# A transformer block with a selective scan: one of two convolved chunks goes from VectorE to TensorE, and steps of the hand-written schedule are placed elsewhere

## Chip, cores and metric

The kernel runs on one core of a Trainium2 chip. The metric is the device time of one execution in microseconds. TensorE, VectorE, ScalarE, GpSimd and SyncE are called PE, DVE, ACT, POOL and SP, as in the profile; PEld is PE's loading of weights. The five engines each work through a queue of their own, in order, and wait for each other by semaphores.

## What is computed

Four sequences of 256 tokens with 512 features go through two layers. The first layer (latent attention beside a gated feed-forward) is untouched by the change. The second layer adds a selective state-space block and a mixture of low-rank experts to its input:

```python
proj = hidden_states @ in_proj_w                 # 512 -> 2 x 1024
x, z = jnp.split(proj, 2, axis=-1)               # both then [batch, 1024, 256]
xp = jnp.pad(x, ((0, 0), (0, 0), (K - 1, 0)))    # K = 4
xc = conv_b[None, :, None]
for k in range(K):
    xc = xc + conv_w[None, :, k:k+1] * xp[:, :, k:k+Lq]
xc = silu(xc)
ssm_p = einsum('bdl,ed->ble', xc, x_proj_w)      # -> dt_r (32), B (16), C (16), each normalised
dt = softplus(einsum('blr,dr->bdl', dt_r, dt_proj_w) + dt_bias)
# scan over time: h = exp(dt * A) * h + dt * B * x ;  y = sum_n h * C
y = (ys + D_param * xc) * silu(z)
out = einsum('bdl,hd->blh', y, out_proj_w)
```

The experts' part is a dense product of the same normalised input, a router (softmax over 8 experts, the two best kept) and rank-16 products weighted by it. The part in question is the convolution: four taps along time, with one weight per channel and tap.

## The kernel before

The first layer fills the first 40% of the time and is bound by PE. Its last products run into the beginning of the scan.

**Tiling of the second layer.** The 1024 channels are eight chunks `c` of 128 partitions; two chunks form a pair `p`. The 16 states of a chunk are taken in four groups, so a chunk has four *steps* and a sequence `PER` = 32. Step `u` of 128 belongs to sequence `u // 32`; `u % 32` is called its place below.

**One step.** ACT forms the decays of step `u + 2` (`decays`, four instructions on L930, into one of three buffers); DVE multiplies the B rows with dt·x (`scan_in`, bx on L936) and scans (`scan`, h on L951); POOL multiplies h with the C rows (hc on L955, in the same function); PE sums the states of step `u - 1` into `ysum` (`states_sum`, L967, with the D part on L965 first in each chunk). Two steps after a chunk's last step DVE closes it (`close_chunk`, L971): `ysum` times the SiLU of z, written over the chunk's `xc`. There are two buffers of h, three of hc, one `ysum`.

**Side work.** While sequence `b` is scanned, the next one, `nxt`, is prepared. Small functions do this, each put to a place by hand: `put(b, place, function, ...)` lists it ahead of the place's scan, `put_late` behind it. Within an engine the order of these lists is the order of the queue. They are: `norm_*` (layer norm), `px_mm` (product with the x half of `in_proj_w`, L737), `conv_in` and `conv_taps` (the convolution of a pair), `conv_silu` (SiLU over all eight chunks, and of a z gate), `pp_mm`, `pp_square`, `pp_norm` (the projection to dt, B and C and its norm), `step_in`, `step_exp`, `step_out` (softplus of dt), `step_x` (dt times x), `spread` (dt and dt·x out to DRAM and back in another layout), `c_rows` and `b_rows`. For sequence `b` itself there are `pz_mm` (z product, L898) with `gate_silu`, and every second sequence `router`, `route_exp`, `route`. For the block's output there are `dense`, `expert_out`, `expert_turn`, `out_mm` (one chunk of `out_proj`, L1059) and `out_x`, which copies the result on ACT and has SP store it; the second half of a sequence's rows is finished early in the next sequence, the first half through the next sequence's places 4 to 15.

**The convolution of a pair.** `conv_in` works on ACT: it copies the product `px` into a padded buffer (`pad`, L745), multiplies both chunks with their last tap and adds the bias (L748, the first chunk in place in PSUM, the second into `xc`), and multiplies the second chunk with its three other taps (`tap`, L753). One place later, `conv_taps` adds the rest: DVE has three multiply-adds for the first chunk (L761), POOL three additions for the second (L767). The pairs of `nxt` stand at places 8, 10, 12 and 14 (`conv_in`) and 9, 11, 13 and 15 (`conv_taps`); while sequence 0 is scanned, one place later. Sequence 0's own convolution runs before the scan begins, with these two functions for its first three pairs and lines of its own for the last.

**PSUM.** All products but `ysum`, the B rows and bx share a pool of three buffers (tag `mm`). An output accumulator `po` holds one from `dense` to `out_x`, a z product from `pz_mm` to `gate_silu`, a px product from `px_mm` until its convolution has read it.

Of the kernel before, what the change touches and what calls it, by code (L numbers as in the profile page):

```python
# [8 lines left out]
F32 = mybir.dt.float32  # L9

F32R = mybir.dt.float32r
AF = mybir.ActivationFunctionType
ALU = mybir.AluOpType
# [4 lines left out]
P = 128  # L18
B, S, D = 4, 256, 512
# [6 lines left out]
DIN, NST, KC, RK = 1024, 16, 4, 32  # L26
# [11 lines left out]
V_CW, V_CB, V_DB, V_AL, V_D, V_END = 0, 4, 5, 6, 22, 23  # L38
# [3 lines left out]
def block_kernel(  # L42
# [24 lines left out]
    nc = tc.nc  # L67
    mm = nc.tensor.matmul
# [15 lines left out]
    ident = cst[:, C_ID : C_ID + P]  # L84
# [34 lines left out]
    live = {}  # L119
# [619 lines left out]

    def conv_in(b, p):  # L740

        px = live["px", b, p]
        if p == 0:
            xcs[b] = (act if b % 3 else w1).tile([P, DC, S], F32, tag=f"xc{b % 3}", name="xc")
        nc.scalar.copy(pads[p % 2][:, :, KC - 1 :], px)  # L745
        for i in range(2):
            v = vec[:, 2 * p + i, :]
            nc.scalar.activation(xcs[b][:, 2 * p + 1, :] if i else px[:, 0, :], px[:, i, :],  # L748
                                 AF.Identity, bias=v[:, V_CB : V_CB + 1],
                                 scale=v[:, V_CW + KC - 1 : V_CW + KC])  # L750
        tp = w1.tile([P, KC - 1, S], F32, tag="tap", name="tap")
        for k in range(KC - 1):
            nc.scalar.activation(tp[:, k, :], pads[p % 2][:, 1, k : k + S], AF.Identity,  # L753
                                 scale=vec[:, 2 * p + 1, V_CW + k : V_CW + k + 1])
        live["tap"] = tp

    def conv_taps(b, p):

        px, c = live["px", b, p], 2 * p
        for k in range(KC - 1):  # L760
            nc.vector.scalar_tensor_tensor(  # L761
                px[:, 0, :] if k < KC - 2 else xcs[b][:, c, :], pads[p % 2][:, 0, k : k + S],
                vec[:, c, V_CW + k : V_CW + k + 1], px[:, 0, :], ALU.mult, ALU.add,
            )
        xc = xcs[b][:, c + 1, :]
        for k in range(KC - 1):
            nc.gpsimd.tensor_tensor(xc, xc, live["tap"][:, k, :], ALU.add)  # L767
# [415 lines left out]
    def put(b, s, f, *a):  # L1183
        at.setdefault(b * PER + s, []).append((f, a))
# [5 lines left out]
    for b in range(B):  # L1190
        nxt = b + 1
        if b:
            put(b, 0, b_rows, b, 1)
            put(b, 0, spread, "du", b, 1)

            for c in range(DC):
                put(b, c // 2, out_mm, b - 1, 1, c)
            put(b, 3, out_x, b - 1, 1)
            put(b, 4, dense, b - 1, 0, 0)
            put(b, 5, dense, b - 1, 0, 1)  # L1200
            put(b, 5, expert_out, b - 1, 0)
            for c in range(DC):
                put(b, 6 + c, out_mm, b - 1, 0, c)
            put(b, 15, out_x, b - 1, 0)
        else:
            put(b, 1, one_out, 2)
            put(b, 1, one_step, 3)
            put(b, 2, one_out, 3)
            put_late(b, 2, load_z, b, 0)
            put_late(b, 2, lambda: send("dt", 0, 1, dts[0, 0][:, 2:4, :]))  # L1210
            put_late(b, 2, step_x, b, 1)
            put(b, 4, load_z, b, 1)
            for k, n in enumerate(("rl", "bw", "lb", "ow")):
                put(b, 9 + 2 * k, load_late, n)
            for p, u in ((0, 3), (1, 8)):
                for i in range(2):
                    put(b, u, pz_mm, b, p, i)
            put(b, 4, gate_silu, b, 0)
            put(b, 12, gate_silu, b, 1)
            put_late(b, 1, add_last, 5)  # L1220
            put_late(b, 3, add_last, 6)
            put_late(b, 4, add_last, 7)
# [15 lines left out]
            put(b, 4 * c - 4 + o, spread, "du", b, c)  # L1238
        put(b, 10, load_z, b, 2)
        put(b, 12, load_z, b, 3)  # L1240
        for p, at_i, at_g in ((2, (14, 15), 16), (3, (19, 21), 23)):
            for i in range(2):
                put(b, at_i[i], pz_mm, b, p, i)
            if p == 3 or nxt == B:
                put(b, at_g, gate_silu, b, p)
        if nxt < B:
            o = 0 if b else 1
            put(b, 0 if b else 2, norm_stats, nxt)
            put(b, 2 if b else 4, norm_scale, nxt)
            put(b, 3 if b else 5, norm_turn, nxt, 0)  # L1250
            (put if b else put_late)(b, 4 if b else 5, norm_copy, nxt, 0)
            put(b, 4 if b else 5, norm_turn, nxt, 1)
            (put if b else put_late)(b, 5, norm_copy, nxt, 1)
            for p in range(NP):
                put(b, 2 * p if b else (5, 6, 9, 9)[p], load_x, nxt, p)
                for i in range(2):
                    put(b, 6 + o + 2 * p + i, px_mm, nxt, p, i)
                put(b, 8 + o + 2 * p, conv_in, nxt, p)
                put(b, 9 + o + 2 * p, conv_taps, nxt, p)
            put(b, 16 + o, conv_silu, nxt, (b, 2))  # L1260
            put(b, 17 + o, pp_mm, nxt, 0)
# [12 lines left out]
            put(b, 27, spread, "dt", nxt, 0)  # L1274
            put(b, 29, spread, "du", nxt, 0)
            put(b, 30, step_x, nxt, 1)
            put(b, 30, b_rows, nxt, 0)
            put(b, 31, spread, "dt", nxt, 1)
            put(b, 23, load_z, nxt, 0)
            put(b, 25, load_z, nxt, 1)  # L1280
            for k, u in enumerate((27, 28, 29, 31)):
                put(b, u, pz_mm, nxt, k // 2, k % 2)
            if b % 2 == 0:
                for i, u in enumerate((16, 17, 18, 20)):
                    put(b, u, router, b, i)
                put(b, 22, route_exp, b)
                put(b, 24, route, b)
            put(b, 25, expert_turn, b)
            put(b, 25, dense, b, 1, 0)
            put(b, 26, dense, b, 1, 1)  # L1290
            put(b, 27, expert_out, b, 1)
        else:

            put(b, 12, expert_turn, b)
            put(b, 17, dense, b, 0, 0)
            put(b, 18, dense, b, 0, 1)
            put(b, 18, expert_out, b, 0)
            put(b, 20, dense, b, 1, 0)
            put(b, 21, dense, b, 1, 1)
            put(b, 21, expert_out, b, 1)  # L1300
# [138 lines left out]
```

## Time and profile before

| | us |
|---|---|
| timed runs | 865.05, 856.58, 862.01 (median 862.01) |
| profiled execution | 866.83 |
| its span, first to last instruction | 865.1 |
| mean granted PE clock | 0.918 |

| engine | busy us of the span | share | instructions |
|---|---|---|---|
| PE | 736.6 | 85% | 3702 |
| DVE | 685.6 | 79% | 684 |
| ACT | 526.5 | 61% | 1011 |
| POOL | 489.6 | 57% | 377 |

Over 40 equal slices of the span (21.6 us each; a digit is the busy share in tenths, 9 is 90% or more):

```profile
PE   5989998989999999897877997677988778957965
DVE  4687755477734437778999999999999999999995
ACT  4315574224556377687794877794976784955451
POOL 3223331001333335569759699669699659697664
```

From slice 20 on DVE is full nearly throughout. POOL and ACT swing between a half and full. The groups of a profile line are read as: line of the kernel, engine, operation, output<-inputs, shapes, count | busy time, mean duration of one | idle time ahead of them and who ended it.

### The profile page before, as it was taken

The numbers are of one execution on the slowest core, as the hardware profiler recorded it, in microseconds if no ns is written. First come the engines' busy times: TensorE is split into PE (matmuls) and PEld (weight loads), VectorE is DVE, ScalarE is ACT, GpSimd is POOL, SyncE is SP. The second block draws the span as 40 slices with busy tenths as digits, with TensorE's granted clock in tenths as the row PEclk, the third lists the DMA queues.
The fourth block names the chain that finished last, engine by engine and source line by source line (L and its number), as shares of the span: only waits on it lengthen the run. The fifth ranks groups of instructions, "written<-read, shape, count | busy, mean of one in ns | idle before, by whom it ended". The sixth has DMA issues, their size and how long they took to land.

```text
span 865.1 us, 10769 instructions
## 1 busy us (share of the span) xinstructions
PE 736.6 (85%) x3702; PEld 411.7 (48%) x3702; DVE 685.6 (79%) x684; ACT 526.5 (61%) x1011; POOL 489.6 (57%) x377
## 2 busy tenths in 40 slices
PE   5989998989999999897877997677988778957965
PEld 3665544666555667554433454334345434312422
DVE  4687755477734437778999999999999999999995
ACT  4315574224556377687794877794976784955451
POOL 3223331001333335569759699669699659697664
PEclk9999999989999999987879899779999878988995
DMA  7234322001233323547532556233535233326200
GB/s 219 76 83 123 95 76 61 1 1 37 74 86 86 104 42 86 137 134 227 161 98 85 147 146 147 85 98 111 167 101 156 76 97 106 101 77 181 73 25 24
DMA packets 67200, 86.68 MB, mean 100 GB/s; under 512 B 12061, under 2 KB 52009, under 8 KB 66762
## 3 DMA queue, kind: packets, MB, share of 16 engines
q1 hardware_dynamic: 57786, 67.12, 27.9%
q0 software_dynamic: 9072, 18.35, 7.6%
q8 instruction: 29, 0.48, 0.2%
q10 hardware_dynamic: 288, 0.52, 0.2%
q14 instruction: 25, 0.20, 0.1%
HBM read 66.58 MB, written 10.22 MB: 89 GB/s over the span
## 4 chain that ended last, share of the span: by engine, by line
PE 42%; DVE 34%; ACT 10%; POOL 7%; issue 5%; DMA 1%; DVEq 0%; SPq 0%; ACTq 0%; POOLq 0%
DVE h L951 20%; DVE bx L936 6%; PE pg L429 6%; PE pu L429 6%; ACT decay L930 6%; PE po L454 4%; POOL hc L955 4%; PE av L382 4%; PE px L737 3%; PE pz L898 2%; PE scT L371 2%; PE ysum L967 2%; DVE mpl L339 2%; PE po L1059 2%; PE pp L781 2%
## 5 line engine op out<-in xcount | busy, mean ns | idle before, releaser
L955 POOL TENSOR_TENSOR hc<-h,cr 128x1024 f32<-128x1024 f32 (+1 forms) x131 | 302.2, 2310 | 103.3 <-DVE h L951 85.5
L951 DVE TENSOR_TENSOR_SCAN h<-decay,bx 128x1024 f32<-128x1024 f32 (+1 forms) x129 | 288.0, 2234 | 15.6 <-PE po L454 4.0
L930 ACT ACTIVATE decay<-dts,aneg 128x255 f32<-128x255 f32 x504 | 213.5, 498 | 118.9 <-DVE h L951 108.5
L967 PE MATMUL ysum<-hc,stack 128*32 128x256 f32 x1024 | 93.8, 437 | 79.6 <-POOL hc L955 79.2
L936 DVE TENSOR_TENSOR bx<-brow,dus 128x1024 f32<-128x1024 f32 x128 | 157.6, 1231 | 3.7
L441 POOL TENSOR_TENSOR hlo<-g,hhi 128x512 fp32r<-128x512 f32 x28 | 35.9, 1281 | 119.9 <-ACT hhi L440 119.9
L967 PEld LDWEIGHTS ysum<-hc,stack 128*32 128x32 f32 x1024 | 22.0, 114 | 142.7 <-POOL hc L955 123.4
L339 DVE TENSOR_REDUCE mpl<-sc 128x4 f32<-128x1024 f32 x64 | 76.7, 1219 | 12.5 <-PE sc L337 12.3
L412 POOL DMA_DIRECT2D wgu<-in_wgu x56 | 31.2, 557 | 96.9 <-PE pg L429 94.8
L373 ACT ACTIVATE pe<-scT 128x1024 f32<-128x1024 f32 x64 | 64.0, 1023 | 23.4 <-PE sc L337 15.1
L1059 PE MATMUL po<-ow,xc 128*128 128x512 f32 x128 | 73.0, 680 | 2.2 <-DVE xc L971 2.2
L898 PE MATMUL pz<-xn1T,w_in 128*128 128x256 f32 x256 | 68.0, 413 | 0.0
L737 PE MATMUL px<-xn1T,w_in 128*128 128x256 f32 x256 | 65.8, 406 | 0.8 <-ACT xn1T L729 0.8
L737 PEld LDWEIGHTS px<-xn1T,w_in 128*128 128x128 f32 x256 | 51.6, 204 | 19.3 <-issue 9.1
L898 PEld LDWEIGHTS pz<-xn1T,w_in 128*128 128x128 f32 x256 | 49.1, 201 | 19.2 <-issue 12.2
L437 DVE SCALAR_TENSOR_TENSOR g<-g,pg 128x512 f32<-128x512 f32 x28 | 19.2, 687 | 41.6 <-ACT g L436 41.6
L454 PE MATMUL po<-wd,hhi 128*128 128x512 f32 x112 | 50.6, 452 | 0.0
L429 PE MATMUL pu<-xhi,wgu 128*128 128x512 f32 x112 | 48.2, 431 | 1.8 <-DMA wgu<-in_wgu 1.8
L429 PE MATMUL pg<-xhi,wgu 128*128 128x512 f32 x112 | 48.7, 435 | 0.0
L440 ACT CAST hhi<-g 128x512 fp32r<-128x512 f32 x28 | 17.3, 619 | 48.8 <-DVE g L439 48.8
L454 PE MATMUL po<-wd,hlo 128*128 128x512 f32 x112 | 45.4, 405 | 0.0
L429 PE MATMUL pu<-xlo,wgu 128*128 128x512 f32 x112 | 45.2, 403 | 0.0
(223 smaller groups left out, 1218.5 us busy)
## 6 DMA issues: line engine op xcount, KB each, us to landing
dts<-dtd SPq DMA_DIRECT2D x124, 128.0 KB, 2.8
dus<-dud SPq DMA_DIRECT2D x124, 128.0 KB, 3.0
wgu<-in_wgu POOLq DMA_DIRECT2D x56, 256.0 KB, 2.8
w_in<-in_inx SPq DMA_DIRECT2D x16, 512.0 KB, 4.4
w_in<-in_inz SPq DMA_DIRECT2D x16, 512.0 KB, 5.5
dtd<-dt SPq DMA_DIRECT2D x15, 256.0 KB, 2.2
dud<-du SPq DMA_DIRECT2D x15, 256.0 KB, 2.2
wd<-in_wd POOLq DMA_DIRECT2D x7, 512.0 KB, 3.5
```

The source lines that it names most:

```text
L339: nc.vector.tensor_reduce(mpl2[b % 2][:, qb, 2 * hp : 2 * hp + 2, 16 + 2 * gq : 18 + 2 * gq], sc.rearrange("p i (f k) -> p i f k", f=2), A ...
L373: nc.scalar.activation(pes[b, k][:, 2 * t : 2 * t + 2, :], sc, AF.Exp)
L429: mm(ps, lhsT=wgus[i][:, hc, :], rhs=xs[j][:, hc, :], start=(hc == 0 and j == 0), stop=(hc == HC - 1 and j == 1))
L454: mm(po, lhsT=hids[th][j][:, m, i * P : (i + 1) * P], rhs=wd[:, m, :], start=False, stop=(m == MC - 1 and j == 1))
L737: mm(px[:, i, :], lhsT=w[:, i, hc, :], rhs=xns[b][:, hc, :], start=(hc == 0), stop=(hc == HC - 1))
L898: mm(pz[:, i, :], lhsT=w[:, i, hc, :], rhs=xns[b][:, hc, :], start=(hc == 0), stop=(hc == HC - 1))
L930: nc.scalar.activation(da[:, k, 1:], live["dts", b, c][:, k, 1:], AF.Exp, scale=aneg[:, c, k, g : g + 1])
L936: nc.vector.tensor_tensor(bx, brow[g // 2][:, g % 2, :].unsqueeze(1).to_broadcast([P, NG, S]), live["dus", b, c], ALU.mult)
L951: nc.vector.tensor_tensor_scan(h[:, n].rearrange("p n t -> p (n t)"), da[:, n].rearrange("p n t -> p (n t)"), bx[:, n].rearrange("p n t -> ...
L955: nc.gpsimd.tensor_tensor(hc[:, n], h[:, n], crows[b][:, g, :].unsqueeze(1).to_broadcast([P, NG // parts, S]), ALU.mult,)
L967: mm(ysum[k * NB : (k + 1) * NB, :], lhsT=stack, rhs=hc[:, k, :], start=False, stop=(g == NU - 1))
L1059: mm(live["po", b, i], lhsT=xcs[b][:, c, i * P : (i + 1) * P], rhs=late_w["ow"][:, c, :], start=False, stop=(c == DC - 1))
```

## The change

Four things.

The first chunk of a pair, from the convolution of sequence 1 on (`b > 0` in `conv_in` and `conv_taps`), is no longer built by one ACT instruction and three DVE instructions. ACT makes four 128x128 diagonal matrices `dg` from the identity, one for each tap, PE multiplies them with the four shifted views of the padded buffer into the PSUM place of the first chunk's product, and ACT copies the sum out with the bias. The instructions of the second chunk stay. For `b == 0` the old instructions stay, but ACT's in-place product of the first chunk now follows the three taps of the second.

The first half's output products (`out_mm`) of chunks 2 to 7 go from places 8 to 13 to places 16 to 21, and `out_x` from 15 to 23, except in the last sequence.

The z product of pair 3 goes from places 19 and 21 to 22 and 24, its gate from 23 to 25.

In sequences 0 and 2 the four router products go from places 16, 17, 18, 20 to 16, 19, 20, 21, `route_exp` from 22 to 23, `route` from 24 to 25; `expert_turn` goes from 25 to 26 and the second half's `expert_out` from 27 to 28 (both in all but the last sequence).

```diff
     def conv_in(b, p):
         px = live["px", b, p]
...
         nc.scalar.copy(pads[p % 2][:, :, KC - 1 :], px)
-        for i in range(2):
-            v = vec[:, 2 * p + i, :]
-            nc.scalar.activation(xcs[b][:, 2 * p + 1, :] if i else px[:, 0, :], px[:, i, :],
-                                 AF.Identity, bias=v[:, V_CB : V_CB + 1],
-                                 scale=v[:, V_CW + KC - 1 : V_CW + KC])
+        v = [vec[:, 2 * p + i, :] for i in range(2)]
+        nc.scalar.activation(xcs[b][:, 2 * p + 1, :], px[:, 1, :], AF.Identity,
+                             bias=v[1][:, V_CB : V_CB + 1], scale=v[1][:, V_CW + KC - 1 : V_CW + KC])
         tp = w1.tile([P, KC - 1, S], F32, tag="tap", name="tap")
         for k in range(KC - 1):
             nc.scalar.activation(tp[:, k, :], pads[p % 2][:, 1, k : k + S], AF.Identity,
-                                 scale=vec[:, 2 * p + 1, V_CW + k : V_CW + k + 1])
+                                 scale=v[1][:, V_CW + k : V_CW + k + 1])
         live["tap"] = tp
+        if b == 0:
+            nc.scalar.activation(px[:, 0, :], px[:, 0, :], AF.Identity, bias=v[0][:, V_CB : V_CB + 1],
+                                 scale=v[0][:, V_CW + KC - 1 : V_CW + KC])
+        else:
+            dg = live["dg"] = w1.tile([P, KC, P], F32, tag="dg", name="dg")
+            for k in range(KC):
+                nc.scalar.activation(dg[:, k, :], ident, AF.Identity, scale=v[0][:, V_CW + k : V_CW + k + 1])

     def conv_taps(b, p):
         px, c = live["px", b, p], 2 * p
-        for k in range(KC - 1):
-            nc.vector.scalar_tensor_tensor(
-                px[:, 0, :] if k < KC - 2 else xcs[b][:, c, :], pads[p % 2][:, 0, k : k + S],
-                vec[:, c, V_CW + k : V_CW + k + 1], px[:, 0, :], ALU.mult, ALU.add,
-            )
+        if b == 0:
...
+        else:
+            for k in range(KC):
+                mm(px[:, 0, :], lhsT=live["dg"][:, k, :], rhs=pads[p % 2][:, 0, k : k + S],
+                   start=(k == 0), stop=(k == KC - 1))
+            nc.scalar.activation(xcs[b][:, c, :], px[:, 0, :], AF.Identity,
+                                 bias=vec[:, c, V_CB : V_CB + 1])
...
             for c in range(DC):
-                put(b, 6 + c, out_mm, b - 1, 0, c)
-            put(b, 15, out_x, b - 1, 0)
+                put(b, 6 + c if c < 2 or nxt == B else 14 + c, out_mm, b - 1, 0, c)
+            put(b, 15 if nxt == B else 23, out_x, b - 1, 0)
...
-        for p, at_i, at_g in ((2, (14, 15), 16), (3, (19, 21), 23)):
+        for p, at_i, at_g in ((2, (14, 15), 16), (3, (22, 24), 25)):
...
-                for i, u in enumerate((16, 17, 18, 20)):
+                for i, u in enumerate((16, 19, 20, 21)):
                     put(b, u, router, b, i)
-                put(b, 22, route_exp, b)
-                put(b, 24, route, b)
-            put(b, 25, expert_turn, b)
+                put(b, 23, route_exp, b)
+                put(b, 25, route, b)
+            put(b, 26, expert_turn, b)
             put(b, 25, dense, b, 1, 0)
             put(b, 26, dense, b, 1, 1)
-            put(b, 27, expert_out, b, 1)
+            put(b, 28, expert_out, b, 1)
```

More of the change, by code (lines that the diff above doesn't have):

```diff
@@ L753, in conv_in @@
             nc.scalar.activation(tp[:, k, :], pads[p % 2][:, 1, k : k + S], AF.Identity,
-                                 scale=vec[:, 2 * p + 1, V_CW + k : V_CW + k + 1])
+                                 scale=v[1][:, V_CW + k : V_CW + k + 1])
         live["tap"] = tp
+        if b == 0:
[5 more added lines that the diff above has]
+                nc.scalar.activation(dg[:, k, :], ident, AF.Identity, scale=v[0][:, V_CW + k : V_CW + k + 1])
     def conv_taps(b, p):
         px, c = live["px", b, p], 2 * p
-        for k in range(KC - 1):
-            nc.vector.scalar_tensor_tensor(
-                px[:, 0, :] if k < KC - 2 else xcs[b][:, c, :], pads[p % 2][:, 0, k : k + S],
-                vec[:, c, V_CW + k : V_CW + k + 1], px[:, 0, :], ALU.mult, ALU.add,
-            )
+        if b == 0:
+            for k in range(KC - 1):
+                nc.vector.scalar_tensor_tensor(
+                    px[:, 0, :] if k < KC - 2 else xcs[b][:, c, :], pads[p % 2][:, 0, k : k + S],
+                    vec[:, c, V_CW + k : V_CW + k + 1], px[:, 0, :], ALU.mult, ALU.add,
+                )
+        else:
[4 more added lines that the diff above has]
+                                 bias=vec[:, c, V_CB : V_CB + 1])
         xc = xcs[b][:, c + 1, :]
```

## The prediction

> **What bounds the kernel now.** I read the page first (busy shares, costliest groups), then the stretches, then the timelines of POOL and PE, then who waited for whom. All times below are in the profiled execution: span 865.1 us, 866.83 us as a run; the three timed runs have the median 862.01 us, 4.8 us lower, so I make the sum against 866.83 and carry the difference over to 862.01.
>
> But for one reordering at 300 us, the change touches the scan half only, from about 380 us on. It has 128 steps; step u issues scan u (counted from 0), and u mod 32 is its place. "Sequence 1" below means: while sequence 1 is scanned. The page's costliest groups:
>
> ```profile
> L955 POOL TENSOR_TENSOR hc<-h,cr 128x1024 f32<-128x1024 f32 (+1 forms) x131 | 302.2, 2310 | 103.3 <-DVE h L951 85.5
> L951 DVE TENSOR_TENSOR_SCAN h<-decay,bx 128x1024 f32<-128x1024 f32 (+1 forms) x129 | 288.0, 2234 | 15.6 <-PE po L454 4.0
> ```
>
> Per step DVE does bx (1.23) and a scan (2.29): scans follow every 3.69 us, 3.80 with a close (L971). POOL's hc is 2.31 of every step before it does anything else. The taps that go:
>
> ```profile
> L761 DVE SCALAR_TENSOR_TENSOR px<-pad,vec,px x30: 462/490/491, 302.2 to 666.4; 128x256 f32<-128x256 f32 x30
> L761 DVE SCALAR_TENSOR_TENSOR xc<-pad,vec,px x15: 481/481/481, 303.3 to 666.9; 128x256 f32<-128x256 f32 x15
> ```
>
> Now the stretch of sequence 1 with all four of its tap groups, and POOL in it:
>
> ```profile
> core 0: us, PE busy (x) PEld busy (x) DVE busy (x) ACT busy (x) POOL busy (x), PEclk, DMA share, GB/s
> 500.75:544.02 43.27, 35.05 (x192) 20.12 (x190) 41.87 (x35) 31.48 (x74) 41.81 (x31) 1.00 0.53 135
> ```
>
> ```profile
> 516.70 1.28 POOL L866 TENSOR_TENSOR e<-e,lw 128x512 f32<-128x512 f32 x1
> 517.93 2.35 POOL L767 TENSOR_TENSOR xc<-xc,tap 128x256 f32<-128x256 f32 x3
> 520.23 2.35 POOL L955 TENSOR_TENSOR hc<-h,cr 128x1024 f32<-128x1024 f32 x1
> ...
> 527.32 2.35 POOL L767 TENSOR_TENSOR xc<-xc,tap 128x256 f32<-128x256 f32 x3
> 529.62 4.67 POOL L955 TENSOR_TENSOR hc<-h,cr 128x1024 f32<-128x1024 f32 x2
> ```
>
> DVE and POOL are both full here: 41.87 and 41.81 of 43.27. POOL has no idle from 509.58 to 539. DVE looks like the bound, but POOL is 0.1 us behind it.
>
> **What is removed.** 36 taps leave DVE (3 for each of 4 pairs in sequences 1 to 3, issued during 0 to 2). A step with taps took 4.95 us against 3.66 without: 1.30 a pair, 15.5 for 12. Of DVE's other waits
>
> ```profile
> DVE xc L971 <- PE ysum L967: 5.8, 2, 4.7
> DVE px L761 <- ACT xc L748: 2.1, 2, 1.7
> DVE nrm L795 <- ACT rs L693: 1.3, 2, 1.0
> ```
>
> the second goes with the taps: 17.6 us at most. What is late next decides.
>
> **POOL is next (sequences 1 and 2).** The order of POOL's instructions does not change. Scan u reuses the h that hc(u-2) reads (two buffers), and the close before scans 41, 45, 49 needs the ysum of hc(39), hc(43), hc(47). From the end of an hc to the scan behind its close took 1.11 us where nothing else was late (hc ended 594.22, scan 61 began 595.33). POOL cannot end hc(43) before 531.95 (529.62 + 2.33), since it had no idle to give: scan 45 begins at 533.06 at the earliest, against 533.28 now. Two pairs' 2.6 us buy 0.2. From there POOL's load thins out, and three steps of 3.69 and one of 3.80 put scan 49 at 547.9, against 549.33: 1.4 us saved of 5.2. Sequence 2 has the same rows 126.8 us later, but a router product (1.19) and an output product (1.13) now stand before ysum(79) on PE: scan 81 at 675.0 against 676.11.
>
> **The additions.** Per pair ACT gets four 128x128 diagonals and one 128x256 eviction and loses one 128x256. No row has the diagonal's form: below it is the 128x136 copy (0.27), above it the 128x256 tap (0.43 from start to start). I take 0.32, nearer the copy since the tap is twice as wide: 4 x 0.32 + 0.5 - 0.54 = +1.25 a pair, +5 per sequence (bounds 4 to 7) on 31.48 busy of 43.27: hidden under the POOL-bound steps; uncovered it would be 15 us. PE gets four 128x256 products a pair, as px (1.9 to 2.0), +7.8, and six output products (1.13) leave the same stretch: hidden on that count. But they stand in front of ysum in PE's queue.
>
> **Sequence 0: a chain through PE takes over.** Here the steps are one later, so the last product group and the first router come at place 16, ahead of ysum(15), which the close before scan 17 needs. The stretch on PE:
>
> ```profile
> 402.14 1.08 PE L967 MATMUL ysum<-hc,stack 128*32 128x256 f32 x8 [2.85 <-POOL hc L955]
> 403.16 3.78 PE L898 MATMUL pz<-xn1T,w_in 128*128 128x256 f32 x8
> 406.73 2.74 PE L737 MATMUL px<-xn1T,w_in 128*128 128x256 f32 x8
> 409.41 0.64 PE L967 MATMUL ysum<-hc,stack 128*32 128x256 f32 x8
> 409.98 1.99 PE L898 MATMUL pz<-xn1T,w_in 128*128 128x256 f32 x8
> ```
>
> POOL still delivers hc(12) at 402.1 (it is full there too). Then in queue order: ysum 1.08 and pz 3.7 (to 406.9), the third pair's products at px's 2.55 (409.5), px 1.95 (411.4); ACT evicts the third pair and makes the due decays first (1.7, to 411.7), then pad 0.6, xc 0.55, taps 1.3, diagonals 1.3 (415.45); each product waits for its own diagonal, so 0.5 more; router 1.19, ysum 0.64, close and scan 0.45: scan 17 at 418.2, against 417.87 now and 415.3 by POOL alone. All of this sequence's 7.3 us is gone. Behind it, two router products leave the path from SiLU to pp_norm, so its 1.0 us wait goes: scan 21 at about 433.5 against 434.11, -0.6.
>
> A rule to weigh: PE after a 2.85 us wait ran slow (pz 3.78 against 1.99), after a 2.42 us wait (at 532.0) it did not. The Trainium skill, TensorE: Matmul & The Clock Gate, "What's actually happening", has the array fall back to half clock only after an idle window of about 3.4 us. By it the 3.2 us wait for hc(12) would leave PE fast, and the sum would be some 2.4 us lower (1.8 on pz, 0.6 on the products behind it). The row says otherwise, and I go by the row.
>
> **The moved steps.** Outputs at places 16 to 21 stand before pp and ysum. Sequence 1: SiLU ends at 549.6 (now 549.13: the eviction and a decay group are ahead of it). PE has waited 1.8 us, under 2.42, so pp runs at 1.9 per half; with the output products (1.13 each) the squares' product ends at 558.3, rs at 559.2, before scan 52 ends (561.3). No wait; the 1.4 is kept. The output accumulator holds one of three PSUM buffers to place 23, which leaves one for pdt and pcr: ACT waits some 1.2 us for pcr at place 22. But SiLU of the last gate (two table loads and 0.6, 3.2 us) now follows step_exp: e is ready at 575.8, against 578.7, so POOL no longer lags at places 24 to 28, and the 1.1 us wait before scan 61 goes: 592.7 against 595.33, -2.6 in all. Sequence 2: the norm is in time, scan 85 at 690.3 against 691.61, -1.3. The routing (4.6 us of DVE) moves from place 24 to 25: the same work, POOL and ACT idle beside it either way: 0. On SP the output's transfer now waits for ACT's place 23 with the next z weights behind it; they are needed four steps (14.8 us) later and land in 5.5: 0; uncovered, 2 us a sequence. POOL's queue is unmoved. In sequence 0's own convolution ACT makes px last, 1.8 us later: the third px product needs the first px buffer, free at 304.85 instead of 303.77, and PE wants it at 304.67: +0.2.
>
> Sum: +0.2 - 0.6 - 2.6 - 1.3 = -4.3 us: 862.5 in this execution's terms, 857.7 from the median.
>
> **The rivals.**
> - Full saving: POOL follows DVE after all. 15.5 + 2.1 + 1.3 + 1.1 = 20 us, 842. Against it: POOL's unbroken row. A milder form, PE never late and only POOL in the way, gives 2.6 + 1.0 in sequence 0, 2.6 and 1.7 after: 7.9, 854.
> - Slower: PE late for the closes. If PE is cold at the diagonals' products of sequence 0 (3.7 where I take 0.5 after the last diagonal), scan 17 comes at 421.4: +3.5, less the 1.0 wait. If pp of sequences 1 and 2 is cold (3.67 as now, not 1.9), pp_norm and the close before scan 85 come late: sequence 1 falls to -0.1, sequence 2 to +1.0. With +0.2: +3.6, 865.6. It decides once PE has waited 2.4 to 2.85 us before those groups. Were all six closes in the convolutions 2 us late, it would be 12 more, 877.
> - Nothing moves: the gains at scans 17, 49, 81 are given back by ACT, which at places 20 to 24 is within 3 us of its due times: 862.
>
> **How the numbers follow.** The forecast with its milder form 0.54, full saving 0.13, nothing 0.10, slower 0.23. About 1% (8.6 us) can be told from no change. Faster by more: the full saving, and 0.08 of the milder form with the spread of the runs (856.58 to 865.05): 0.21. Slower by more: the heavier part of the PE rival: 0.15. Range 849 to 869: it holds the forecast, the milder form, nothing, and PE late once; left out are full saving and PE late at every close.
>
> **What would show it.** Right: no L761 taps after 381 us; DVE busy falls by some 17 us while its idle before L971 or before scans grows by about as much; POOL unbroken at places 5 to 13 of sequences 1 and 2, with hc(43) ending within 0.3 us of 531.95; the wait before scan 61 gone. Wrong: scan 45 two or more us early (POOL not the bound), ysum waits behind diagonals in sequences 1 or 2, or scan 17 before 416 or after 420.

## The result, and the profile after

| | before | changed |
|---|---|---|
| median of 20 timed runs each, taken side by side, us | 864.15 | 860.73 |
| lowest and highest, us | 856.58, 868.9 | 857.88, 864.88 |
| ratio to before, 95% interval | | 0.9977, 0.9955 to 1.0000 |
| profiled execution: span, us | 865.1 | 857.2 |
| mean granted PE clock | 0.918 | 0.950 |

So the change takes off 2.0 us, between 3.9 and nothing. (The two medians lie 3.4 us apart and the two means 2.0; the ratio goes with the means. Ratios and intervals, here and below, leave out the few runs in a slower state, three of e4's nine.) The forecast was 4.3. A second measurement (12 runs, in the experiments) gave 0.9975, 0.9945 to 1.0005. The profiled executions differ by some 7.8 us; most of that is not the change, as the table of stretches below will show.

The costliest groups of the profile after keep their order; POOL's hc and DVE's scan cost what they did:

```profile
L967 POOL TENSOR_TENSOR hc<-h,cr 128x1024 f32<-128x1024 f32 (+1 forms) x131 | 302.4, 2312 | 102.5 <-DVE h L963 81.1
L963 DVE TENSOR_TENSOR_SCAN h<-decay,bx 128x1024 f32<-128x1024 f32 (+1 forms) x129 | 288.0, 2234 | 20.2 <-POOL hc L967 4.7
```

DVE's idle ahead of the scans grew from 15.6 to 20.2 us, and POOL's hc has become the first that ends it. The instructions by their lines (shortest, median and longest in ns, first and last start) show no tap of line 767 on DVE after 313 us, and the three additions of the change:

```profile
L767 DVE SCALAR_TENSOR_TENSOR px<-pad,vec,px x6: 489/490/490, 303.0 to 311.6; 128x256 f32<-128x256 f32 x6
L773 PE MATMUL px<-pad,dg x96: 377/379/796, 382.5 to 662.5; 128*128 128x256 f32 x96
L761 ACT ACTIVATE dg<-cst,vec x48: 384/392/398, 382.0 to 659.4; 128x128 f32<-128x128 f32 x48
L775 ACT ACTIVATE xc<-px,vec x12: 456/474/475, 384.8 to 662.9; 128x256 f32<-128x256 f32 x12
```

POOL in the convolution places of sequence 1:

```profile
518.12 2.35 POOL L967 TENSOR_TENSOR hc<-h,cr 128x1024 f32<-128x1024 f32 x1
520.43 1.27 POOL L887 TENSOR_TENSOR du<-dt,xc 128x512 f32<-128x512 f32 x1
521.65 2.34 POOL L779 TENSOR_TENSOR xc<-xc,tap 128x256 f32<-128x256 f32 x3
523.95 4.68 POOL L967 TENSOR_TENSOR hc<-h,cr 128x1024 f32<-128x1024 f32 x2
528.60 2.33 POOL L779 TENSOR_TENSOR xc<-xc,tap 128x256 f32<-128x256 f32 x3
...
533.52 2.38 POOL L967 TENSOR_TENSOR hc<-h,cr 128x1024 f32<-128x1024 f32 x1 [0.27 <-DVE h L963]
```

It is still unbroken, to 533.25. The first of the two hc at 523.95 is hc(43), ended at 526.28. Scan 40 stands 5.63 us earlier than before, so that is 531.91 in the times of before; the forecast said 531.95. Who waited for whom on DVE in the scan half (total, times, longest):

```profile
DVE xc L983 <- PE ysum L979: 13.0, 7, 2.9
...
DVE h L963 <- POOL hc L967: 4.7, 5, 1.8
...
DVE w L1010 <- ACT ex L1020: 3.0, 1, 3.0
```

Counted alike, with the last close of all in it, the first row was 8.4 in three waits before (the 5.8 in two of the prediction leave that close out). Two of its new waits, 2.87 and 2.88 us, stand ahead of scans 45 and 77; e4 below, which has neither the taps nor the new products, has 2.86 at both, so there DVE waits for POOL's hc through `ysum`. The last row did not exist. It is the first tensor of `route`. Here is what it waited for, on ACT:

```profile
691.23 0.59 ACT L822 COPY cr<-pcr 128x512 f32<-128x512 f32 x1 [1.22 <-PE pcr L819]
...
693.32 0.57 ACT L1076 COPY x<-po 128x512 f32<-128x512 f32 x1
693.79 1.06 ACT L846 ACTIVATE u<-u 128x1024 f32<-128x1024 f32 x1
...
698.11 0.57 ACT L822 COPY cr<-pcr 128x512 f32<-128x512 f32 x1
698.58 0.23 ACT L1020 ACTIVATE ex<-ex 128x32 f32<-128x32 f32 x1
```

and on DVE:

```profile
693.57 2.29 DVE L963 TENSOR_TENSOR_SCAN h<-decay,bx 128x1024 f32<-128x1024 f32 x1
698.84 0.20 DVE L1010 TENSOR_REDUCE w<-ex 128x4 f32<-128x32 f32 x1 [2.99 <-ACT ex L1020]
```

The exponential takes 0.23 us, but at place 23 it is issued behind `step_exp`: ACT's queue holds four activations (4.3 us), a copy of the output and a copy of C rows ahead of it. DVE had its scan done at 695.86 and sat until 698.84.

**Where the time went.** The scan starts give each stretch its length, whatever the first layer did. All numbers are differences of scan start times in the traces, in us; the experiments are described below.

| scans | before | changed | changed, again | e1 | e2 | e3 | e4 | e5 | e6 | e7, r2 | e8, r3 |
|---|---|---|---|---|---|---|---|---|---|---|---|
| 9 to 40 (seq. 0) | 129.96 | 127.55 | 128.37 | 128.31 | 128.46 | 128.97 | 126.87 | 123.05 | 128.37 | 128.93, 127.53 | 125.89, 130.14 |
| 40 to 49 (seq. 1) | 38.49 | 37.05 | 37.49 | 37.37 | 37.07 | 38.69 | 37.04 | 33.48 | 37.48 | 37.05, 37.05 | 36.59, 36.59 |
| 49 to 72 | 88.29 | 87.94 | 89.35 | 89.23 | 88.85 | 87.77 | 88.24 | 91.96 | 89.34 | 87.15, 87.15 | 88.10, 90.90 |
| 72 to 81 (seq. 2) | 38.49 | 37.08 | 39.18 | 37.67 | 37.07 | 38.69 | 37.03 | 33.49 | 39.19 | 37.06, 37.76 | 36.81, 36.83 |
| 81 to 127 | 176.11 | 178.63 | 179.54 | 178.06 | 176.79 | 178.46 | 175.65 | 178.23 | 175.90 | 175.75, 175.90 | 176.09, 176.09 |
| sum, 9 to 127 | 471.34 | 468.25 | 473.93 | 470.64 | 468.24 | 472.58 | 464.83 | 460.21 | 470.28 | 465.94, 465.39 | 463.48, 470.55 |

In the profile of the changed kernel the stretches of the change are 3.1 us shorter than before. Another 3.4 of the 7.8 come at scan 9: a wait for `ysum` in front of that close was 4.72 us before and 1.32 after. That is not the change: the two executions of e8 and r3, which are the same kernel, waited 3.88 and 1.17 there. It goes with PE's granted clock just ahead of it: half for 10.2 us in the four profiles with a wait of 3.87 us or more (before, e2, e5, e8), for 3.4 us in the nine others. The last 1.5 us lie behind scan 127, where the same four output products took 3.78 us before and 2.27 after; scan 0 began 0.2 us later. (Over all thirteen profiles scan 0 begins between 330.6 and 334.9 us, with versions of both kernels early and late, so whole spans can't be compared to a few us.)

### The profile page after: what moved, and what is told of

The parts are those of the page before. It is cut to its first block, busy times and chain, and to the rows that moved or that the text cites. A ratio compares the mean times of both kernels' runs of the same rounds, so it can differ in the third digit from the quotient of the medians.

```text
span 857.2 us, 10979 instructions
## 1 busy us (share of the span) xinstructions
PE 740.2 (86%) x3798; PEld 422.5 (49%) x3798; DVE 670.8 (78%) x648; ACT 536.9 (63%) x1059; POOL 489.7 (57%) x377
## 4 chain that ended last, share of the span: by engine, by line
PE 41%; DVE 24%; ACT 14%; POOL 10%; issue 6%; DMA 3%; SPq 1%; DVEq 0%; ACTq 0%; POOLq 0%
DVE h L963 14%; ACT decay L942 6%; PE pu L429 6%; PE pg L429 6%; POOL hc L967 5%; DVE bx L948 4%; PE av L382 4%; PE pz L910 3%; PE px L737 2%; PE scT L371 2%; PE ysum L979 2%; PE po L1071 2%; PE po L454 2%; DVE mpl L339 2%; POOL xc L779 1%
## 5 line engine op out<-in xcount | busy, mean ns | idle before, releaser
L963 DVE TENSOR_TENSOR_SCAN h<-decay,bx 128x1024 f32<-128x1024 f32 (+1 forms) x129 | 288.0, 2234 | 20.2 <-POOL hc L967 4.7
L979 PE MATMUL ysum<-hc,stack 128*32 128x256 f32 x1024 | 89.5, 416 | 59.9 <-POOL hc L967 59.7
L1071 PE MATMUL po<-ow,xc 128*128 128x512 f32 x128 | 70.2, 657 | 2.2 <-DVE xc L983 2.2
L910 PE MATMUL pz<-xn1T,w_in 128*128 128x256 f32 x256 | 71.2, 428 | 0.0
L737 PE MATMUL px<-xn1T,w_in 128*128 128x256 f32 x256 | 61.0, 384 | 0.9 <-ACT xn1T L729 0.8
L910 PEld LDWEIGHTS pz<-xn1T,w_in 128*128 128x128 f32 x256 | 51.1, 209 | 20.2 <-issue 11.6
L737 PEld LDWEIGHTS px<-xn1T,w_in 128*128 128x128 f32 x256 | 47.6, 190 | 13.8 <-issue 3.9
L440 ACT CAST hhi<-g 128x512 fp32r<-128x512 f32 x28 | 17.3, 619 | 50.1 <-DVE g L439 50.1
L429 PE MATMUL pg<-xlo,wgu 128*128 128x512 f32 x112 | 44.3, 396 | 0.0
```

The source lines that it names most:

```text
L429: mm(ps, lhsT=wgus[i][:, hc, :], rhs=xs[j][:, hc, :], start=(hc == 0 and j == 0), stop=(hc == HC - 1 and j == 1))
L737: mm(px[:, i, :], lhsT=w[:, i, hc, :], rhs=xns[b][:, hc, :], start=(hc == 0), stop=(hc == HC - 1))
L910: mm(pz[:, i, :], lhsT=w[:, i, hc, :], rhs=xns[b][:, hc, :], start=(hc == 0), stop=(hc == HC - 1))
L963: nc.vector.tensor_tensor_scan(h[:, n].rearrange("p n t -> p (n t)"), da[:, n].rearrange("p n t -> p (n t)"), bx[:, n].rearrange("p n t -> ...
L979: mm(ysum[k * NB : (k + 1) * NB, :], lhsT=stack, rhs=hc[:, k, :], start=False, stop=(g == NU - 1))
L1071: mm(live["po", b, i], lhsT=xcs[b][:, c, i * P : (i + 1) * P], rhs=late_w["ow"][:, c, :], start=False, stop=(c == DC - 1))
```

## The experiments

Theory A: the moved routing makes DVE wait for ACT. Theory B: POOL, not DVE, paces the convolution places, and so the taps were worth little. Theory C: the z products at places 22 and 24 take back the gain before scan 61. The rival to them is that the new products and diagonals on PE and ACT ate the gain.

### e1_route22: the exponential one place earlier

```diff
-                put(b, 23, route_exp, b)
+                put(b, 22, route_exp, b)
```

> The changed kernel with route_exp put at place 22 instead of 23, so that ex stands ahead of step_exp's four activations (4.35 us) in ACT's queue; route stays at place 25. Theory A (the moved routing makes DVE wait): the 2.99 us wait before line 1010 in step 88 goes and nothing of it comes back, about 2.9 us below the changed kernel, 4.9 us below the kernel before (ratio about 0.994). Rival (the scan is held at that place by something else, ACT's decays or POOL's hc, and the wait before line 1010 only shows it first): a wait of about the same size appears before the next scans, and the time stays the changed kernel's (ratio 0.998).

Measured: 860.37 us against 861.08, ratio 0.9991 (0.9964 to 1.0019). Missed. The wait before L1010 went, but another came three steps earlier, on DVE:

```profile
688.19 0.18 DVE L1018 TENSOR_REDUCE m<-ml 128x4 f32<-128x32 f32 x1 [1.22 <-ACT ml L996]
688.41 1.11 DVE L1019 TENSOR_TENSOR ex<-ml,m 128x32 f32<-128x32 f32 x1
```

`route_exp` begins on DVE, and the last router's logits are made at place 21: at place 22 they are not copied out yet, 1.22 us, and the subtraction took 1.11 us where it takes 0.19 in the changed kernel. It ended at 689.52, just behind the hc that POOL worked on (to 689.47); the last section comes back to that. From scan 81 to 127 only 0.6 us came off. The routing sits in a gap between its router and its `route`, and both edges are sharp. That the wait could move from one edge to the other is what made the next version (e6).

### e2_conv and e3_place: the two halves of the change

e2 is the convolution alone with every `put` as before; e3 is the kernel before with the `put` lines of the change alone.

> The convolution on TensorE alone, every step placed as in the kernel before (output products at places 8 to 13, out_x at 15, last gate at 23, routers at 16, 17, 18, 20, route_exp at 22, route at 24). Theory B (POOL's hc and its side work pace the convolution places of sequences 1 and 2, so the removed taps buy about 1.4 us a sequence there): scan 49 and scan 81 come again 1 to 1.5 us earlier than in the kernel before, not 5; by theory A there is no wait before line 1010, so that this kernel is 1 to 4 us below the kernel before (ratio 0.995 to 0.999), at or below the whole change. Rival (the output products had to leave, PE is the bound with the diagonals' products): ysum comes late for the closes before scans 41, 45, 49, 73, 77, 81 by 1 us or more each, and it is 3 us or more above the kernel before (ratio 1.003 and up).

> The moved steps alone: the convolution with VectorE's taps as before, all placements as in the change. Theory A: DVE waits some 3 us for ex before line 1010 in sequence 2 here too, with pp_norm's 1.0 us wait in sequence 0 gone and about 0.3 of the wait before scan 61: 1 to 2 us above the kernel before (ratio 1.001 to 1.002). Rival (the wait for ex comes from the convolution's new load on ACT): no such wait, 1 to 2 us below the kernel before (ratio 0.998).

Measured: e2 859.11 us against 861.08, ratio 0.998 (0.9958 to 1.0002). As theory B has it, the stretches 40 to 49 and 72 to 81 shrink by 1.4 us each, exactly as with the whole change, and no wait stands before L1010. The rival, 1 us or more at each close and a slower kernel, is out: the closes in the convolution places are not later than in the whole change, and the two waits of 2.9 us for `ysum`, before scans 45 and 77, are in e4 too, which has none of the new products. e2's sum over scans 9 to 127 (468.24) equals that of the whole change (468.25).

e3: 862.46 us, ratio 1.0012 (0.998 to 1.0043), in the trace 1.2 us above before, with the wait in it and no product of the new convolution anywhere:

```profile
698.42 0.20 DVE L998 TENSOR_REDUCE w<-ex 128x4 f32<-128x32 f32 x1 [2.32 <-ACT ex L1008]
```

So the wait belongs to the moved steps. They gain in the stretch 49 to 72 (0.5) and at `pp_norm`, and lose 2.35 from scan 81 on. The timed ratios alone could not tell e2 from e3; the stretches do.

### e4_notaps and e5_nopool: the load on DVE, the load on POOL

e4, in the kernel before: the three taps are skipped for b > 0, and ACT's product with the last tap goes straight to `xc`. e5, in the changed kernel: the three additions are skipped. Each leaves out a part of the convolution.

```diff
 e4
...
-        for k in range(KC - 1):
+        for k in range(KC - 1 if b == 0 else 0):
             nc.vector.scalar_tensor_tensor(
...
 e5
-        for k in range(KC - 1):
+        for k in range(KC - 1 if b == 0 else 0):
             nc.gpsimd.tensor_tensor(xc, xc, live["tap"][:, k, :], ALU.add)
```

> The kernel before with the three taps of the first chunk left out for sequences 1 to 3 and nothing in their place (ScalarE's product with the last tap goes straight to xc): it leaves that part of the convolution out. The taps' 15.5 us of DVE then cost nothing anywhere else, so this is the most that their removal can buy with the steps placed as before. Theory B (POOL paces these places): scan 45 at most 0.5 us earlier against its sequence's first close, scan 49 and 81 by 1 to 2 us, sequence 0 by up to 3.6 us: 5 to 7 us in all (ratio 0.992 to 0.994). Rival (DVE was the bound and TensorE's products took its place): 12 to 20 us (ratio 0.977 to 0.986).

> The changed kernel with POOL's three additions of the second chunk (2.35 us a pair) left out for sequences 1 to 3: it leaves that part of the convolution out; TensorE's and ScalarE's parts stay. Theory B (POOL paces the convolution places): from scan 40 to scan 49 DVE alone would need 9 x 3.69 + 3 x 0.11 = 33.5 us, against 38.5 before and 37.05 after the change; about 3.5 us come off in sequence 1, as much in sequence 2 and 1 to 3 in sequence 0, so 8 to 10 us below the changed kernel (ratio to the kernel before 0.986 to 0.989). Rival (PE's queue of px, diagonals' products and ysum is the bound beside POOL): scan 49 stays within 1 us of the changed kernel's, 2 us or less in all.

Measured: e4 856.4 us (median of all nine runs) against 861.08, ratio 0.993 (0.9896 to 0.9964), the stretches 40 to 49 and 72 to 81 at 37.04 and 37.03. The changed kernel has 37.05 and 37.08 there. So the products, diagonals and evictions cost nothing in these places in that profile; what the taps' removal could buy was 1.4 in each, and the change got it all.

e5: 850.84 us against 861.8, ratio 0.9866 (0.9814 to 0.9917). With POOL's 2.35 us a pair gone, the stretches fall to 33.48 and 33.49; 33.5 was forecast for DVE alone. The engines' busy time in scans 40 to 49 (columns: stretch, length, then PE, PEld, DVE, ACT, POOL with the number of instructions; PE clock, DMA share, GB/s), before, changed and e5:

```profile
510.84:549.33 38.49, 26.98 (x152) 15.58 (x152) 37.42 (x33) 28.47 (x61) 35.81 (x27) 0.94 0.57 143
```

```profile
505.21:542.26 37.05, 30.68 (x170) 20.08 (x168) 32.48 (x21) 30.72 (x75) 35.77 (x27) 0.95 0.53 136
```

```profile
502.66:536.14 33.48, 29.18 (x169) 18.89 (x168) 32.38 (x21) 30.98 (x75) 27.37 (x15) 1.00 0.53 150
```

DVE's 37.42 of 38.49 became 32.48 of 37.05: 4.9 us of work gone, 1.4 us of time. In the second row POOL has 35.77 of 37.05 and is the fullest; in the third DVE is full again, and the waits before scans 45 and 77 are gone. PE has more work in the second and third rows than in the first, and is nowhere full. Not everything stays gained: in e5 the close in step 56 waited 4.78 us for `ysum`, 4.0 more than in the changed kernel.

### e6_exfirst and e7_pz: routing and z product put right

```diff
 e6
+            if b % 2 == 0:
+                put(b, 23, route_exp, b)
             put(b, 23, step_exp, nxt, 0)
...
-                put(b, 23, route_exp, b)
                 put(b, 25, route, b)
 e7, besides
-        for p, at_i, at_g in ((2, (14, 15), 16), (3, (22, 24), 25)):
+        for p, at_i, at_g in ((2, (14, 15), 16), (3, (22, 23), 25)):
```

> The changed kernel with route_exp still at place 23, but issued ahead of step_exp there, so that ex stands in ACT's queue before step_exp's four activations and the second cr copy (4.9 us), while its logits (ml, late by 1.2 us when route_exp stood at place 22) are long there. Theory A: no wait before line 1010 nor before line 1018, so the 2.99 us lost from scan 85 to scan 89 of sequence 2 stay gained: 2.9 us below the changed kernel, ratio to the kernel before 0.9945. Rival (something else holds that stretch and gives a wait of the same size elsewhere, as in the run before): 0.998.

> As the run before, with the second half of the last z pair at place 23 instead of 24, so that its eight matmuls (3.78 us when slow) no longer stand in PE's queue right ahead of the ysum that the close before scan 57 waits for. Theory C (this order on PE is what took back two thirds of the 1.1 us gained before scan 61): the wait before line 983 in step 56 (0.76 us) goes, and sequence 1 is 0.7 us shorter; ratio 0.9935 to 0.994. Rival (the late ysum comes from pcr, which has to wait for ACT to free the one PSUM buffer, wherever pz stands): the wait stays, and nothing changes.

Measured, e6: 857.15 us against 861.8, ratio 0.9926 (0.9895 to 0.9958). ACT of e6:

```profile
698.30 0.56 ACT L1076 COPY x<-po 128x512 f32<-128x512 f32 x1
698.77 0.23 ACT L1020 ACTIVATE ex<-ex 128x32 f32<-128x32 f32 x1
698.90 1.05 ACT L846 ACTIVATE u<-u 128x1024 f32<-128x1024 f32 x1
```

The exponential ends at 699.00, DVE's scan at 700.07, and `route` begins at 700.18 without a wait. The stretch 81 to 127 is 175.90, against 178.63 and 179.54 in the two profiles of the changed kernel: 2.7 and 3.6 us, all of it. Theory A holds. The sum over scans 9 to 127 of this one profile (470.28) does not show the gain against the first profile of the changed kernel, since PE was slow at two other places in it (as in r1 below); against the second, which has the same slow places, it is 3.65 us.

e7: 856.43 us, ratio 0.9943 (0.9914 to 0.9972). Timed, it cannot be told from e6. In the trace the wait in step 56 (0.76 and 2.17 us in the two profiles of the changed kernel, 2.17 in e6) is gone, and the stretch 49 to 72 is 87.15. r2, the same kernel, has 87.15 again. PE around it, in the changed kernel and in r2:

```profile
565.24 2.07 PE L819 MATMUL pcr<-nrm,bcsel 64*128 64x256 f32 x4
567.24 1.08 PE L979 MATMUL ysum<-hc,stack 128*32 128x256 f32 x8
568.25 3.78 PE L910 MATMUL pz<-xn1T,w_in 128*128 128x256 f32 x8
571.96 0.68 PE L979 MATMUL ysum<-hc,stack 128*32 128x256 f32 x8
```

```profile
565.15 3.63 PE L910 MATMUL pz<-xn1T,w_in 128*128 128x256 f32 x8
568.70 1.14 PE L819 MATMUL pcr<-nrm,bcsel 64*128 64x256 f32 x4
569.77 1.07 PE L979 MATMUL ysum<-hc,stack 128*32 128x256 f32 x16
```

In the first the last `ysum`, for which the close waits, ends at 572.6, behind a slow z product; in r2, with the z product (slow as well) one place earlier, the second of two `ysum` ends at 570.8. That is as theory C has it, and its size would be 0.8 us against one profile and 2.2 against the other. But PE's pace differed as well. The granted clock at this place was 0.50 for 6.8 us in the first profile of the changed kernel and for 10.2 in r1 and e6, for only 3.4 in r2, and 1.00 throughout in e7. And with the z product at place 23 the wait came back where PE was slow for longer: 0.40 us in e8 (half clock for 6.8 us) and 3.15 in r3 (two spells of 6.8 us, around and ahead of these groups). So place and pace both bear on it, and theory C is shown only in part.

### e8_bal: a tap of the second chunk goes to DVE

Besides e7's edits, for b > 0 DVE makes the tap k = 0 of the second chunk, ACT prepares and POOL adds two.

```diff
...
+        if b:
+            nc.vector.scalar_tensor_tensor(xc, pads[p % 2][:, 1, 0:S], vec[:, c + 1, V_CW : V_CW + 1], xc,
+                                           ALU.mult, ALU.add)
-        for k in range(KC - 1):
+        for k in range(1 if b else 0, KC - 1):
             nc.gpsimd.tensor_tensor(xc, xc, live["tap"][:, k, :], ALU.add)
```

> As the run before, and VectorE makes one of the three taps of each pair's second chunk (0.43 us of DVE a pair), so that POOL adds two instead of three (1.57 instead of 2.35 us) and ScalarE prepares two. Theory B: POOL gives 0.78 us a pair and DVE has 0.43 to lose: 1 to 1.8 us off in sequence 1 and in sequence 2 up to scan 49 and 81, up to 1 us in sequence 0, 2 to 4.5 us below the run before (ratio 0.989 to 0.992). Rival (DVE and POOL are level, so that what one gives the other takes; or PE's queue is next): within 0.5 us of the run before.

Measured: 856.96 us, ratio 0.995 (0.9917 to 0.9984), level with e7. The stretches 40 to 49 and 72 to 81 are 36.59 and 36.81, 0.5 and 0.25 below e7 where 1 to 1.8 was expected. DVE of e8 in sequence 1, and POOL beside it:

```profile
512.40 1.53 DVE L780 SCALAR_TENSOR_TENSOR xc<-pad,vec,xc 128x256 f32<-128x256 f32 x1
...
521.04 1.66 DVE L780 SCALAR_TENSOR_TENSOR xc<-pad,vec,xc 128x256 f32<-128x256 f32 x1
```

```profile
511.31 2.34 POOL L971 TENSOR_TENSOR hc<-h,cr 128x1024 f32<-128x1024 f32 x1
...
520.07 4.85 POOL L971 TENSOR_TENSOR hc<-h,cr 128x1024 f32<-128x1024 f32 x2
```

Two of the stretch's four taps took 1.53 and 1.66 us instead of 0.46. Each ended 0.2 to 0.3 us after the hc that POOL was working on (513.65; the first of two, about 522.4). What was to cost DVE 0.43 cost it 1.1 to 1.2 more, twice in nine steps. In r3, the same kernel, DVE's tap also waited twice for ACT's `xc` in sequence 0 (1.17 and 1.12), and 3.15 came back at the close of step 56; so e8's stretches sum to 2.5 us less than e7's, and r3's to 5.2 more than r2's.

### The changed kernel again, beside e7 and e8

> The changed kernel itself once more, beside the two that follow on one chip. By the sum of its own stretches in the traces (scan 9 to scan 127, 3.1 us less than the kernel before) ratio 0.9965; if the first measurement of 20 runs stands, 0.9977. The product's pace on TensorE in the close before scan 9 and behind the last scan differs from run to run and moves single profiles by up to 4 us either way.

> ex ahead of step_exp, and the last z pair's second half at place 23, once more. Theories A and C together: 2.9 and 0.8 us below the changed kernel, scan 9 to scan 127 some 5.4 us less than the kernel before, ratio 0.9935 to 0.995. Rival (the two waits were chance of single profiles): level with the changed kernel.

> The same with one of the second chunk's taps on VectorE, once more; its first timing (0.995) did not show the 2.5 us that its trace gained over the run before it (scan 9 to scan 127: 7.9 us less than the kernel before against 5.4). Theory B: 2 to 3 us below the run before, ratio 0.991 to 0.992. Rival (the gain in the scan half is lost elsewhere in most runs, or DVE and POOL are level): no difference to the run before, 0.994 to 0.995.

| | median us | ratio to before (862.26 us) |
|---|---|---|
| changed (r1) | 861.04 | 0.9975 (0.9945 to 1.0005) |
| e7 again (r2) | 855.82 | 0.9910 (0.9876 to 0.9944) |
| e8 again (r3) | 856.78 | 0.9938 (0.9906 to 0.9970) |

The changed kernel comes out as at first. Routing and z product put right take another 5.2 us off it, more than the change itself took off, so that this version beats both kernels. The intervals of r2 and the changed kernel do not overlap, if only just; those of r2 and r3 do, so the rival to e8 stands: no difference.

r1's profile shows what the first one did not. Its stretches sum to 473.93, 2.6 us above before, where the first profile had 3.1 below. PE at the convolution's last but one pair in sequence 2, in the first profile and in r1:

```profile
651.39 0.64 PE L979 MATMUL ysum<-hc,stack 128*32 128x256 f32 x8 [2.61 <-POOL hc L967]
651.96 2.00 PE L773 MATMUL px<-pad,dg 128*128 128x256 f32 x8
653.79 1.89 PE L737 MATMUL px<-xn1T,w_in 128*128 128x256 f32 x8
```

```profile
653.87 1.08 PE L979 MATMUL ysum<-hc,stack 128*32 128x256 f32 x8 [2.60 <-POOL hc L967]
654.88 3.78 PE L773 MATMUL px<-pad,dg 128*128 128x256 f32 x8
658.45 2.74 PE L737 MATMUL px<-xn1T,w_in 128*128 128x256 f32 x8
```

The same kernel and the same 2.6 us of waiting; once PE goes on at full pace, once at half. The granted clock (the 1.00 and the 0.50 in these rows, for the first and for r1) is the difference:

```profile
651.39:654.00 2.61, 2.61 (x17) 1.97 (x18) 1.90 (x2) 1.75 (x6) 2.61 (x2) 1.00 1.10 235
653.87:658.66 4.79, 4.79 (x17) 3.27 (x18) 3.61 (x3) 1.75 (x5) 4.63 (x5) 0.50 1.08 240
```

In r1 the closes before scans 77 and 81 then waited 3.31 and 1.57 us for `ysum` (2.88 and none in the first profile), the convolution ended late, and the wait for `ex` grew to 3.75 us. e6 shows the same slow group at the same place.

## Why the prediction was off

It forecast the right direction (the interval just reaches no change) and about twice the effect. By its own steps:

- **POOL is next: right, to a tenth.** hc(43) at 531.91 against 531.95; scan 45 0.23 us earlier against 0.2; scan 49 1.4 against 1.4; e4 and e5 show the same from either side. The full saving was refused for the right reason. This is the first profile; in r1, where PE was at half pace ahead of the close, scan 45 came 0.2 us later than before and scan 49 gained 1.0.
- **The additions: right.** Four diagonals take 1.26 to 1.27 us against 1.28; a group of products takes 2.0. (The tap's "0.43 from start to start" was its run of three, 1.29 us, divided by three; from start to start it is 0.40, and a diagonal 0.29.) They cost nothing where PE keeps its pace (e4 against the changed kernel). The 36 taps' durations, 17.3 us together, are gone as forecast; DVE's busy time fell by 14.8 only (685.6 to 670.8), since the taps' records had overlapped their neighbours'. The reordering ahead of the scan: the third px product began 0.50 us behind the start of the product ahead of it, at 304.11, instead of 0.23, so 0.27 us against 0.2; scan 0 began 0.18 (first profile) and 0.14 (r1) later.
- **Sequence 0: mis-sized, in the safe direction.** Scan 17 was to come at 418.2 by a chain through a slow PE. From scan 9 on the first profile gains 1.3 us to it, which puts it at 416.6 in the times of before; r1, e1 and e6 0.5, or 417.4. The cause is the row on which this step stood: after a wait of 2.85 us PE was slow before. In the first profile it waited 2.83 us at that place and went on at full pace:

```profile
399.48 0.64 PE L979 MATMUL ysum<-hc,stack 128*32 128x256 f32 x8 [2.83 <-POOL hc L967]
400.05 1.99 PE L910 MATMUL pz<-xn1T,w_in 128*128 128x256 f32 x8
```

  With `pp_norm`'s wait gone as forecast, scan 21 gains 2.4 us (first profile) and 1.6 (r1), against 0.6.
- **The gain before scan 61: mis-sized.** 1.1 us was forecast, the 1.11 us wait did go, and 0.76 came back in step 56 (2.17 in r1): stretch 49 to 72 gained 0.35, or lost 1.06. The step had followed the gate, which moved late, on ACT and POOL, and not the z product, which moved with it, ahead of the `ysum` that the close before scan 57 needs. e3, with the moved steps alone, has the wait there (0.62 us); before, e2 and e4 have none. How much of it is the z product's place and how much PE's pace stays open (e7, r2 and r3).
- **The routing: the step that failed.** "The routing (4.6 us of DVE) moves from place 24 to 25: the same work, POOL and ACT idle beside it either way: 0." It measured 2.99 us, and 3.75 in r1, enough by itself to bring 4.3 down to 1.3. That 3.1 us were left in the first profile is luck: sequence 0 gave 2.4 where 0.6 was forecast and sequence 1 gave 1.8 of 2.6, while from scan 72 on 1.1 were lost where 1.3 were to be gained. `route_exp` had moved too, from 22 to 23, and with it ex on ACT to behind `step_exp`'s four activations, the second copy of C rows and the moved `out_x`. "Idle beside it" was read from the queue before and not from the queue after. In sequence 0 the same order costs nothing: ex ended at 441.99 and DVE took it up at 442.03, which leaves no margin; there is no `out_x` ahead of it, and the C rows' 1.22 us wait on ACT is not there. e3 shows the wait without the new convolution, e6 the stretch without it.
- **The clock, weighed both ways.** The row (slow after 2.85 us, granted clock 0.50; not after 2.42, granted 1.00) was taken as a threshold, and it is none: 2.60 us gave both in two executions of one kernel. The Trainium skill, TensorE: Matmul & The Clock Gate, "What's actually happening", says that the window is free-running and the outcome varies from run to run. That agrees. It also puts the fall to half clock behind an idle window of about 3.4 us; here slow products follow a wait of 2.60 us (r1) and, in e7, one of 1.66 (in sequence 2 the C rows' product took 2.07 us behind it, with the granted clock at 0.51, where it takes 1.13).
- **The rival "PE late for the closes"** was priced as a whole outcome. It is a part of every outcome: r1 and e6 have it in sequence 2, the first profile does not. So one of its signs of being wrong, waits for `ysum` behind the diagonals' products, came true in r1 (1.57 us before scan 81) and not in the first profile.

How often a timed execution, of which only the length is known, has PE slow at these places stays open; so the 2.0 us can't be divided exactly. By the two profiles the change's own stretches lie between 3.1 us less and 2.6 more than in the one profile of before, which had its own slow places.

## What to carry to other kernels

A step that is moved by one place can pass another engine's queue entries: list for each of its instructions, on each engine, what now stands ahead of it, and price it by that, however small the instruction is. Removing work from a full engine is worth what the second fullest leaves; leaving the work out of one engine, and then out of the other, measures both floors in two runs. And where single profiles differ by as much as the effect, compare stretches between fixed marks of the program and not spans.

## What the runs showed of the hardware

PE's pace after a wait is not set by the wait's length alone. The granted clock in the thirteen traces is 1.0 or 0.5 and nothing else, and each of the 464 spells between two changes lasts a whole multiple of 3.41 us; of the 232 at half, 122 last one of these, 84 two, 25 three and one five. Over the same traces, in the scan half, `ysum` groups after a wait were counted by the distance from their fourth to their fifth matmul (0.22 us at full pace, 0.41 at half): after 1.1 us 79 were at full pace and one at half, after 1.8 us 31 and 21, after 2.0 us 25 and none, after 2.6 us 3 and 12, after 3.0 us 8 and 24 (five more changed between). A schedule that leaves PE in such waits ahead of a close has a time that varies from one execution to the next: scans 9 to 127 of the changed kernel took 468.25 and 473.93 us.

A DVE instruction with both tensors in SBUF can last until POOL's current instruction ends, and the profile counts that as its busy time and not as a wait. The second chunk's tap took 1.53 and 1.66 us instead of 0.46 in e8, and up to 2.39 in r3, each time ending 0.3 us behind an instruction of POOL; the subtraction L1019 took 1.11 instead of 0.19 in e1, ending at 689.52, while POOL's hc ran to 689.47. The first chunk's taps, with one operand in PSUM, took 0.46 to 0.49 in the kernel before while POOL was just as full. The Trainium skill, SBUF — State Buffer, "SBUF: two separate sides", has such an instruction of DVE, with two inputs in SBUF, and one of POOL that reads SBUF exclude each other for a whole instruction. The time lost in these cases agrees with it; that the place of the operands alone makes the difference was not tried by itself.
